# A cross-attention block on one core: the statements of the written-out front, up to the ninth step, in a new order

## The chip, the cores and the metric

The kernel runs on one core of one Trainium2 chip. The metric is the device time of one execution in microseconds (us), and lower is better. A core has a matrix engine (PE in the profile; its weight loads are PEld), three engines for elementwise work (DVE, the vector engine; ACT, the scalar engine; POOL, the general one) and a queue (SP) that here only issues DMA transfers. Each engine works off its own list of instructions in the order of the program and waits on semaphores for the others.

## The reference

One transformer block, for 128 sequences of 128 tokens of width 256, in fp32. Queries come from `x`, keys and values from `ctx`; 16 heads of width 16, a strictly causal mask, a softmax, an output projection, a residual and a layer norm, then a two-layer network of width 1024 with its residual and layer norm.

```python
q = (query @ Wq + bq)    # 16 heads of 16
k = (key @ Wk + bk)
v = (values @ Wv + bv)
scores = einsum('bhqd,bhkd->bhqk', q, k) / sqrt(16)
scores = where(j < i, scores, -1e30)
attn = softmax(scores); attn[:, :, 0, :] = 0
ctx = einsum('bhqk,bhkd->bhqd', attn, v)
x1 = layer_norm(query + ctx @ Wo + bo, ln1_g, ln1_b)
out = layer_norm(x1 + relu(x1 @ W1 + b1) @ W2 + b2, ln2_g, ln2_b)
```

## The kernel before

**Pairs and stages.** The 128 sequences are worked in 64 pairs, numbered from 0. A number such as the 3 in `sums(3, 0, ALL)` is the pair. The second argument of the softmax functions is `hi`: 1 for the later half of the queries, which sees up to 128 keys, 0 for the earlier half, which sees 64. A pair goes through these stages:

- `tokens(p, "x" or "c")` turns a loaded block so that features stand on the partitions (DVE, L289); `project_queries`, `project_keys` (PE, L300) and `values` (PE, L356) are the projections, and `copy_queries`, `copy_keys`, `spread_values`, `stack_values` (ACT, L326, L345, L370, L379) bring them out of the PSUM banks.
- `scores` (PE, L411) or, from pair 4 on, `scores_both` (PE, L440) fill the eight banks of PSUM with scores. `mask` (DVE, L456 or L464) takes them out of the banks and adds the mask; a bank is free for PE's next use only then.
- `maximum` is a maximum on DVE (L475) and a subtraction on POOL (L476); `exponential` is ACT (L483); `sums` is a sum and a reciprocal on DVE (L498, L499) and a multiplication on POOL (L500). From pair 5 on there is another softmax: `exponential_by_head` on ACT (L937) does the subtraction and the sum with the exponential, head by head, and POOL is not needed.
- `turn(p, hi, t)` transposes a third of the weights in 32x32 blocks on DVE (L533) into the tile `turned`. `bring(p, queue, which)` and `bring_all` then move the blocks with 16 DMAs (L552), mostly issued by SP, from `turned` to `brought`. A turn of the next pair may overwrite `turned` only after these transfers have landed. `turn_on_pe` (PE, L569, and ACT, L571) does the same for pairs 0 and 1 without DMAs.
- `weigh` (PE, L586, L596) multiplies `brought` with the values, `context` takes the result out, `attention_out` (PE, L635) is the output projection, `attention_sum` and `stats` (DVE, L683, L650) add the residual and take mean and variance, `deviation` and `shift` (POOL, L657, L732; `scale_and_shift` does both for the second norm) make the scales, `norm1` applies them (ACT, L709).
- `hidden` (PE, L875; ACT, L882) and `second` or `second_half` (PE, L894, L1412) are the two-layer network.

From pair 7 on the products are written with 7 block products in place of 8 (a Strassen-like scheme, PE L1153 and L1364). It needs sums and differences of weight blocks: `combine_weights(w, wc)` makes four 128x128 tiles on POOL, `combine_w1` and `combine_w2` four 128x512 tiles each.

**What sets the order.** The whole body is under `tc.manual_schedule`, so the order of the Python statements is the order on each engine. Statements of pairs 9 to 60 come from one list of keys, `ORDER`, in a loop `step(p)`; a step of that loop works at once on the scores of pair p, the output of pair p-2, and the network of pairs p-3 and p-4. The end of the program is written out. So is its front: some 330 statements, in which the pipeline fills. From `do("weigh", 7)` on (`weigh` of pair 5; `do(key, p)` runs one key of the loop) the front is in the loop's own pieces. `do("weigh", 8)` is `weigh` of pair 6, `do("scores", 8)` are the scores of pair 8, `do("v1", 8)` the first products of its values, `do("eh7", 7)` to `do("el7", 7)` are the exponentials of pair 7 by two heads each. The loop begins with `weigh` of pair 7, at about 185 us.

`empty(n)` puts n no-ops on PE. The list holds 5768 of them before and after the change, and the instructions of each engine are the same set in both.

```python
def sums(p, hi, part):                       # L487
    ...
        nc.vector.tensor_reduce(su, sm[:, part, :], AX.X, ALU.add)      # L498
    nc.vector.reciprocal(rs, su)                                        # L499
    nc.gpsimd.tensor_tensor(sm[:, part, :], sm[:, part, :], ..., ALU.mult)   # L500
...
def bring(p, queue, which, whole=False):     # L544
    for u in which:
        i, j = u // NS, u % NS
        queue.dma_start(brought_all[32 * j : 32 * j + 32, i, at],       # L552
                        turned_all[32 * i : 32 * i + 32, ...])
```

Of the kernel before, what the change touches and what calls it, by code (L numbers as in the profile page):

```python
# [10 lines left out]
ALU = mybir.AluOpType  # L11
# [8 lines left out]
def tile_cross_attention_block(  # L20
# [1842 lines left out]
    tokens(2, "x")  # L1863
    scores(0, 1)
# [15 lines left out]
    project_queries(1)  # L1880
    copy_queries(1)
    values(1)
    mask(0, 0, A)
    ps_bv = fold_values()
    maximum(0, 0, ALL)
    sums(0, 1, ONE)
    exponential(0, 0, ALL)
    spread_values(1)
    tokens(2, "c")
    scores(1, 1)  # L1890
    sums(0, 1, TWO)
    stack_values(1)
    sums(0, 0, ALL)
    add_values(ps_bv)
    turn_on_pe(0, 1, range(0, 1))
    turn_on_pe(0, 1, range(1, 2))
    mask(1, 1, A)
    mask(1, 1, B)
    project_keys(2)
    add_bo(0)  # L1900
# [4 lines left out]
    maximum(1, 1, ONE)  # L1905
    scores(1, 0)
    exponential(1, 1, ONE)
    weigh(0)
    context(0)
    project_queries(2)  # L1910
    maximum(1, 1, TWO)
    mask(1, 0, A)
    mask(1, 0, B)
    maximum(1, 0, ALL)
    attention_out(0)
    copy_keys(2)
    exponential(1, 1, TWO)
    values(2)
    sums(1, 1, ONE)
    tokens(3, "c")  # L1920
    copy_queries(2)
    exponential(1, 0, ALL)
    scores(2, 1)
    attention_sum(0)
    stats(0, states[0]["t1"], 1)
    deviation(0, 1)
    stack_values(2)
    shift(0, 1)
    spread_values(2)
    norm1(0)  # L1930
    sums(1, 1, TWO)
    ps_b1 = fold_norm1()
    turn_on_pe(1, 1, range(0, 1))
    turn_on_pe(1, 1, range(1, 2))
    mask(2, 1, B)
    maximum(2, 1, TWO)
    turn_x1_on_pe(0)
    tokens(4, "x")
    nc.gpsimd.tensor_tensor(be1b_r, be1_r, b2_r, ALU.add)
    sums(1, 0, ALL)  # L1940
    mask(2, 1, A)
    turn_on_pe(1, 1, range(2, 3))
    keep_b1(ps_b1)
    add_b1()
    hidden(0, range(2, 4), None, (2, 3, 4, 0))
    exponential(2, 1, TWO)
    maximum(2, 1, ONE)
    hidden(0, range(0, 2), None, (2, 3, 4, 0))
    scores(2, 0)
    turn_on_pe(1, 1, range(3, 4))  # L1950
    tokens(3, "x")
    mask(2, 0, B)
    turn_on_pe(1, 0, range(0, 1))
    mask(2, 0, A)
    add_bo(1)
    maximum(2, 0, ALL)
    sums(2, 1, TWO)
    exponential(2, 1, ONE)
    turn_on_pe(1, 0, range(1, 2))
    sums(2, 1, ONE)  # L1960
    hidden(0, range(4, 6), None, (2, 3, 4, 0))
    project_queries(3)
    copy_queries(3)
    tokens(4, "c")
    exponential(2, 0, ALL)
    project_keys(3)
    sums(2, 0, ALL)
    turn(2, 1, 0)
    turn(2, 1, 1)
    add_bo(3)  # L1970
    turn(2, 0, 0)
    copy_keys(3)
    hidden(0, range(6, 8), None, (2, 3, 4, 0))
    weigh(1)
    bring(2, nc.sync, EVERY[:8])
    context(1)
    residual1(0)
    scores(3, 1)
    mask(3, 1, B)
# [38 lines left out]
    attention_sum(2)  # L2018
    copy_queries(4)
    load_ahead(2)  # L2020
    load_ahead(4)
    stats(2, states[2]["t1"], 1)
    deviation(2, 1)
    turn(3, 1, 0)
    turn(3, 0, 0)
    turn(3, 1, 1)
    shift(2, 1)
    norm1(2)
    hidden(1, range(4, 6), None, (0, 1, 2, 7))
    hidden(1, range(0, 2), None, (0, 1, 2, 7))  # L2030
    hidden(1, range(2, 4), None, (0, 1, 2, 7))
    bring(3, nc.sync, LATE_FIRST[:3])
    turn_x1(2, between=lambda: bring(3, nc.sync, LATE_FIRST[3:7]))
    hidden(1, range(6, 8), None, (0, 1, 2, 7))
    add_bo(4)
    tokens(6, "x")
    combine_w1()
    tokens(5, "c")
    bring(3, nc.sync, LATE_FIRST[7:])
    scores_both(4)  # L2040
    mask(4, 0, A)
# [12 lines left out]
    exponential(4, 1, TWO)
    sums(4, 0, ALL)
    sums(4, 1, TWO)
    second(1, 1)
    second_sum(1)
    hidden(2, range(2, 4), None, (2, 3, 4, 0))
    residual1(2)  # L2060
    turn(4, 0, 0)
    load_ahead(3)
    copy_keys(5)
    copy_queries(5)
    load_ahead(5)
    turn(4, 1, 0)
    weigh(3)
    hidden(2, range(0, 2), None, (2, 3, 4, 0))
    context(3)
    turn(4, 1, 1)  # L2070
    do("stats2", 7)
    stats(0, states[0]["t2"], 2)
    values(4)
    spread_values(4)
    stack_values(4)
    scores_both(5)
    tokens(6, "c")
# [1025 lines left out]
```

## Time and profile before

| what | value |
|---|---|
| median of 3 runs | 1472.59 us (1471.45 to 1474.57) |
| the profiled execution's own time | 1469.98 us |
| its span, first to last instruction | 1468.2 us |
| busy share of PE, PEld, DVE, ACT, POOL | 99%, 95%, 93%, 89%, 87% |
| mean granted clock of PE | 0.997 |
| front, to the first `weigh` of the loop | 184.8 us |
| one step of the loop on PE | 21.97 us |

The profile is of one execution. Its span leaves out 1.8 us around the program. "Busy" of PE includes time in which a matmul is only on its way through the array, so 99% does not say that nothing could be gained; what PE waits for is told by the waits and the idle times in front of instructions. In the timeline a row begins with the start in us and the duration; in brackets at its end stand the idle time of the engine before it and what ended it. SPq is the issue of a DMA on SP's queue, which is over long before the data has landed.

### The profile page before, as it was taken

The page shows a single profiled execution, that of the slowest core. Times are in us where ns is not written, and L with a number is a line of the kernel's source. Part 1 is how long each engine was busy: PE and PEld are TensorE (multiplying, and loading weights), DVE is VectorE, ACT ScalarE, POOL GpSimd, SP SyncE. Part 2 cuts the span into 40 slices and gives each one's busy share as a digit, 9 for nine tenths or more (in the row PEclk, how much of TensorE's full clock was granted, in tenths as well). Part 3 has the DMA queues.
Part 4 walks back from the last instruction along what each step waited for, and adds up shares of the span by engine and source line. Part 5 has one row for each costly group of instructions (what it writes and reads, how often), then busy time and mean ns, then how long its engine had stood idle before and what let it go on. Part 6 is the DMA issues. An engine that isn't in the chain of part 4 may idle for free.

```text
span 1468.2 us, 62017 instructions
## 1 busy us (share of the span) xinstructions
PE 1447.0 (99%) x20713; PEld 1391.6 (95%) x20713; DVE 1371.9 (93%) x3175; ACT 1303.4 (89%) x5559; POOL 1271.2 (87%) x1872
## 2 busy tenths in 40 slices
PE   8999899999999999999999999999999999999998
PEld 7778799999999999999999999999999999999988
DVE  6987999999999999999999999999999999999767
ACT  5659899999999999999999999999999999999743
POOL 5986898988988988988988998998998998998966
PEclk9999999999999999999999999999999999999999
DMA  8274766766766766766766766766766776774541
GB/s 208 63 143 102 179 154 156 162 157 156 161 160 153 162 158 153 163 160 153 160 158 157 159 158 158 160 158 156 163 157 153 163 161 149 164 158 116 140 103 51
DMA packets 367881, 220.34 MB, mean 150 GB/s; under 512 B 280032, under 2 KB 335584, under 8 KB 367584
## 3 DMA queue, kind: packets, MB, share of 16 engines
q1 hardware_dynamic: 365296, 214.27, 63.8%
q8 instruction: 187, 3.06, 1.0%
q10 hardware_dynamic: 2288, 2.11, 0.7%
q14 instruction: 110, 0.90, 0.2%
HBM read 55.06 MB, written 18.09 MB: 50 GB/s over the span
## 4 chain that ended last, share of the span: by engine, by line
PE 92%; DVE 4%; POOL 1%; DMA 1%; ACT 1%; issue 1%; SPq 0%; DVEq 0%; ACTq 0%; POOLq 0%
PE banks L1153 48%; PE banks L1364 24%; PE banks L440 6%; PE banks L596 4%; PE banks L586 2%; PE banks L300 2%; PE banks L875 2%; PE banks L977 1%; PE banks L635 1%; PE banks L356 1%; DVE sm L464 1%; ACT sm L937 1%; DVE turned L533 1%; PE banks L1050 0%; PE banks L1412 0%
## 5 line engine op out<-in xcount | busy, mean ns | idle before, releaser
L937 ACT ACTIVATE sm<-banks,nmx 128x128 f32<-128x128 f32 x944 | 340.8, 396 | 17.9 <-DVE nmx L1568 14.7
L937 ACT ACTIVATE sm<-sm,nmx 128x64 f32<-128x64 f32 x944 | 325.2, 384 | 1.5 <-DVE nmx L926 1.5
L937 ACT ACTIVATION_READ_ACCUMULATOR sm<-banks,nmx 128x1 f32 x944 | 222.8, 236 | 0.0
L937 ACT ACTIVATION_READ_ACCUMULATOR sm<-sm,nmx 128x1 f32 x944 | 221.8, 235 | 0.0
L533 DVE STREAM_TRANSPOSE turned<-sm 128x1024 f32<-128x1024 f32 x186 | 217.0, 1214 | 3.3 <-DMA brought<-turned 1.8
L1153 PE MATMUL banks<-wt,hS 128*128 128x128 f32 x1344 | 177.7, 275 | 0.0
L1364 PE MATMUL banks<-xS,w1t 128*128 128x128 f32 x1344 | 177.2, 275 | 0.0
L1153 PEld LDWEIGHTS banks<-wt,hS 128*128 128x128 f32 x1344 | 163.6, 192 | 0.1
L1364 PEld LDWEIGHTS banks<-xS,w1t 128*128 128x128 f32 x1344 | 163.4, 192 | 0.0
L1568 DVE TENSOR_REDUCE nmx<-banks 128x4 f32<-128x512 f32 x224 | 152.3, 680 | 1.9
L1557 POOL TENSOR_TENSOR hS<-hT 128x512 f32<-128x512 f32 x116 | 148.2, 1279 | 3.7 <-ACT hT L882 2.4
L1364 PE MATMUL banks<-brought,w 128*128 128x128 f32 x896 | 118.2, 275 | 0.0
L1153 PE MATMUL banks<-w,hT 128*128 128x128 f32 x896 | 109.8, 275 | 0.0
L1364 PEld LDWEIGHTS banks<-brought,w 128*128 128x128 f32 x896 | 109.0, 192 | 0.0
L1618 POOL TENSOR_TENSOR x1b<-x,g_r 128x512 f32<-128x512 f32 x56 | 72.4, 1293 | 39.4 <-ACT x L709 39.4
L1153 PEld LDWEIGHTS banks<-w,hT 128*128 128x128 f32 x896 | 104.8, 192 | 0.1
L440 PE MATMUL banks<-kT,qT 32*64 32x128 f32 (+1 forms) x3840 | 98.3, 331 | 1.8 <-ACT vz L1278 1.5
L1393 ACT ACTIVATE hT<-hT,b1e_c 128x256 f32<-128x256 f32 x224 | 95.7, 510 | 1.2 <-DVE hT L1389 1.1
L1562 DVE TENSOR_TENSOR banks<-banks,neg 128x256 f32<-128x256 f32 x224 | 93.3, 417 | 0.0
L440 PEld LDWEIGHTS banks<-kT,qT 32*64 32x64 f32 x3840 | 79.4, 131 | 12.6 <-ACT vz L1278 1.9
L709 ACT ACTIVATE x<-t,nb,sd 128x256 f32<-128x256 f32 x126 | 68.4, 593 | 19.7 <-POOL nb L732 12.9
L1219 ACT ACTIVATE kr<-banks,b_c 128x128 f32<-128x128 f32 x224 | 83.7, 411 | 1.7 <-PE banks L1153 1.7
(324 smaller groups left out, 4821.5 us busy)
## 6 DMA issues: line engine op xcount, KB each, us to landing
brought<-turned SPq DMA_DIRECT2D x936, 128.0 KB, 2.4
out_dram<-t SPq DMA_DIRECT2D x63, 256.0 KB, 4.0
xb<-in_x_dram SPq DMA_DIRECT2D x124, 128.0 KB, 3.2
cb<-in_ctx_dram SPq DMA_DIRECT2D x124, 128.0 KB, 3.2
x<-in_x_dram SPq DMA_DIRECT2D x56, 256.0 KB, 2.8
kT<-kr SPq DMA_DIRECT2D x112, 128.0 KB, 2.2
brought<-turned SPq DMA_DIRECT2D x40, 96.0 KB, 2.4
w<-in_L_xattn_W_dram SPq DMA_DIRECT2D x2, 1024.0 KB, 7.4
```

What stands on the lines that cost most here:

```text
L440: nc.tensor.matmul(st["sps", hi][r][s * HP : (s + 1) * HP, m * 2 * n : (m + 1) * 2 * n].rearrange("p (e j) -> p e j", e=2), st["qT"][strip ...
L533: nc.vector.transpose(turned[:, :, at : at + 256].rearrange("p j (n a) -> p n j a", a=32), states[p]["sm", hi].rearrange("p h j -> p (h j) ...
L709: nc.scalar.activation(x1[:, s], t1[:, s], AF.Identity, bias=st["nb", 1][:, s], scale=sd[:, s])
L937: nc.scalar.activation(sm[:, h, :], src, AF.Exp, bias=nmx[:, h : h + 1], scale=1.0, **({"accum_out": st["su"][:, at : at + 1]} if summed e ...
L1153: nc.tensor.matmul(out, left(k) if self.depth > 1 else left, right(k) if self.depth > 1 else right, start=(n == 1 and k == 0), stop=(k == ...
L1219: nc.scalar.activation(self.k[:, m, s * P : (s + 1) * P], src, AF.Identity, bias=bk_c[:, m : m + 1], scale=1.0,)
L1364: nc.tensor.matmul(ps[:, i * P : (i + 1) * P].rearrange("p (n a) -> p n a", a=32), left(i), right, start=(n in (1, 2, 5) and i == 0), stop ...
L1393: nc.scalar.activation(self.hT[:, f, at], self.hT[:, f, at] if src is None else src, AF.Relu, bias=b1e_c[:, f : f + 1], scale=1.0,)
L1557: engine.tensor_tensor(c[:, n], left, right, how)
L1562: nc.vector.tensor_tensor(ps[:, :, HP:], ps[:, :, HP:], neg[:, 1, None, :].to_broadcast([P, 4, HP]), ALU.add)
L1568: nc.vector.tensor_reduce(states[p]["nmx", 1][:, 4 * b : 4 * b + 4], banks[:, b].rearrange("p (n j) -> p n j", j=P), AX.X, ALU.max, negate ...
L1618: nc.gpsimd.tensor_tensor(st["x1b"], st["x1b"] if n else st["x1"], (be1b_r if n else g1_r)[:, None, :].to_broadcast([P, 2, D]), ALU.add if ...
```

## The change

The front's statements, from `tokens(2, "x")` up to the loop, stand in a new order. No statement is added or taken away, no size, engine, tile or bank is changed. On SP's queue every DMA stands where it stood; PE, DVE, ACT and POOL have a new order. The loop and the end of the program are the same. The diff has some 330 statements that move; this is its core, with what the prediction speaks of:

```diff
     tokens(2, "x")
+    combine_weights(wv, wvt)
     scores(0, 1)
...
+    combine_weights(wk, wkt)
     values(0)
     stack_values(0)
+    combine_weights(wo, wot)
...
-    tokens(2, "c")
+    tokens(2, "c")
+    tokens(3, "c")
     exponential(0, 0, ALL)
...
     project_keys(2)
-    add_bo(0)
+    copy_keys(2)
     turn_on_pe(0, 1, range(2, 3))
...
-    sums(3, 1, ONE)
-    exponential(3, 0, ALL)
-    attention_out(2)
-    scale_w1()
-    copy_keys(4)
-    sums(3, 1, TWO)
-    sums(3, 0, ALL)
...
+    second_sum(0)
+    exponential(3, 1, ONE)
+    sums(3, 1, ONE)
+    sums(3, 1, TWO)
+    scale_w1()
+    nc.gpsimd.tensor_tensor(b1e_c, b1e_c, b1_c, ALU.add)
+    stats(0, states[0]["t2"], 2)
+    scale_and_shift(0)
+    exponential(3, 0, ALL)
+    sums(3, 0, ALL)
+    context(2)
+    turn(3, 1, 1)
...
-    turn(3, 1, 0)
-    turn(3, 0, 0)
-    turn(3, 1, 1)
-    shift(2, 1)
+    shift(2, 1)
+    turn(3, 0, 0)
+    project_keys(4, 6)
+    copy_keys(4)
+    turn(3, 1, 0)
...
+    hidden(2, range(4, 6), None, (2, 3, 2, 3))
+    hidden(2, range(6, 8), None, (2, 3, 2, 3))
+    weigh(4)
     project_keys(6)
+    copy_keys(6)
+    values(5)
...
-    values(5)
-    copy_queries(6)
-    turn(5, 1, 1)
-    hidden(2, range(6, 8), None, (2, 3, 2, 3))
-    turn(5, 0, 0)
-    combine_weights(wk, wkt)
-    reciprocals(5)
     turn_x1_blocks(3)
-    weigh(4)
...
+    do("kr", 7)
+    do("ks", 7)
+    do("ks2", 7)
+    do("q4", 7)
+    do("qr", 7)
...
+    do("el0", 7)
+    do("vr", 7)
...
+    do("el1", 7)
+    do("el2", 7)
+    do("el6", 7)
+    do("el5", 7)
+    do("xs0", 7)
     do("weigh", 8)
```

On POOL, which is without work from 5 to 20 us, three of the four `combine_weights` now stand ahead of the first softmax; the fourth, `combine_w1` and `combine_w2` move too. On PE the list changes in few places: `weigh` of pair 4 stands ahead of the keys of pair 6 and the values of pair 5, and the hidden layer, the projections and the scores of pairs 2 to 6 change places with one another.

The places of the two pieces that the prediction speaks of, in the order of the engines' lists. A row is a line of the kernel, the operation, the tiles written and read (a number at the end of a name tells tiles of one kind apart), the size and a count.

The first is on POOL, around the last work of the softmax of pair 3 (`sm_3`; `nmx0` and `rs0` are the maxima and reciprocals of the earlier half, `rs1` those of the later one). Before:

```order
L476 TENSOR_TENSOR sm_3_1017<-sm_3_1017,nmx0_3_1110 128x1024
L500 TENSOR_TENSOR sm_3_1017<-sm_3_1017,rs1_3_0_1199 128x1024
L500 TENSOR_TENSOR sm_3_1017<-sm_3_1017,rs1_3_8_1215 128x1024
L500 TENSOR_TENSOR sm_3_1017<-sm_3_1017,rs0_3_0_1220 128x1024
L657 TENSOR_SCALAR ve1_2_1251<-mv1_2_1244 128x2
L658 TENSOR_TENSOR sd1_2_1252<-ve1_2_1251,power_96 128x2
```

The same place on POOL now, where `b1e_c` is a sum of biases and `ve2_0`, `sd2_0`, `nb2_0` are the scales of pair 0's second norm:

```order
L476 TENSOR_TENSOR sm_3_1000<-sm_3_1000,nmx0_3_1087 128x1024
L500 TENSOR_TENSOR sm_3_1000<-sm_3_1000,rs1_3_0_1221 128x1024
L500 TENSOR_TENSOR sm_3_1000<-sm_3_1000,rs1_3_8_1226 128x1024
L2016 TENSOR_TENSOR b1e_c_185<-b1e_c_185,b1_c_116 128x8
L657 TENSOR_SCALAR ve2_0_1241<-mv2_0_1234 128x2
L658 TENSOR_TENSOR sd2_0_1242<-ve2_0_1241,power_96 128x2
L732 TENSOR_SCALAR nb2_0_1245<-mv2_0_1234,sd2_0_1242 128x1 x2
L500 TENSOR_TENSOR sm_3_1000<-sm_3_1000,rs0_3_0_1249 128x1024
L657 TENSOR_SCALAR ve1_2_1273<-mv1_2_1264 128x2
```

Four small operations, among them the scales of pair 0's second norm, have come in ahead of the third multiplication of `sums` of pair 3.

The second is on PE, where the keys of pair 6 (L300) and the values of pair 5 (L356) stood among the matmuls of the hidden layer of pair 2 (L875, with no-ops between them), ahead of `weigh` of pair 4:

```order
 L875 MATMUL banks<-brought,w_132 128x256
 L253 NO_OP x6
-L300 MATMUL banks<-cT_1633,wk 128x256 x4
-L356 MATMUL banks<-wv,cT_1369 128x256 x4
 L875 MATMUL banks<-brought,w_132 128x256
 L253 NO_OP x6
```

And on PE a little further on, at the end of `weigh` of pair 4 (L586, L596) and the second layer of pair 2 (L1412):

```order
 L586 MATMUL banks<-brought,vd_176 32x64 x8
 L596 MATMUL banks<-brought,vz_174 32x64 x16
+L300 MATMUL banks<-cT_1653,wk 128x256 x4
+L356 MATMUL banks<-wv,cT_1346 128x256 x4
 L1412 MATMUL banks<-w_138,hT 128x256 x8
```

The two projections have moved from ahead of `weigh` of pair 4 to behind it.

More of the change, by code (lines that the diff above doesn't have):

```diff
@@ L1909, in tile_cross_attention_block @@
     context(0)
-    project_queries(2)
-    maximum(1, 1, TWO)
-    mask(1, 0, A)
+    exponential(1, 1, TWO)
     mask(1, 0, B)
     maximum(1, 0, ALL)
+    sums(1, 1, ONE)
+    project_queries(2)
+    copy_queries(2)
     attention_out(0)
[L1916 to L1923, printed above, removed]
     attention_sum(0)
     stats(0, states[0]["t1"], 1)
+    scores(2, 1)
     deviation(0, 1)
+    shift(0, 1)
@@ L1927, in tile_cross_attention_block @@
+    sums(1, 1, TWO)
+    exponential(1, 0, ALL)
+    values(2)
     stack_values(2)
-    shift(0, 1)
     spread_values(2)
     norm1(0)
-    sums(1, 1, TWO)
+    add_bo(1)
+    nc.gpsimd.tensor_tensor(be1b_r, be1_r, b2_r, ALU.add)
     ps_b1 = fold_norm1()
+    mask(2, 1, B)
     turn_on_pe(1, 1, range(0, 1))
     turn_on_pe(1, 1, range(1, 2))
-    mask(2, 1, B)
+    turn_x1_on_pe(0)
+    turn_on_pe(1, 1, range(2, 3))
+    mask(2, 1, A)
+    scores(2, 0)
+    hidden(0, range(2, 4), None, (2, 3, 4, 0))
@@ L1936, in tile_cross_attention_block @@
     maximum(2, 1, TWO)
-    turn_x1_on_pe(0)
+    exponential(2, 1, TWO)
     tokens(4, "x")
-    nc.gpsimd.tensor_tensor(be1b_r, be1_r, b2_r, ALU.add)
-    sums(1, 0, ALL)
-    mask(2, 1, A)
-    turn_on_pe(1, 1, range(2, 3))
-    keep_b1(ps_b1)
-    add_b1()
[L1945 to L1952, printed above, removed]
@@ L1953, in tile_cross_attention_block @@
-    turn_on_pe(1, 0, range(0, 1))
[L1954 to L1958, printed above, removed]
+    tokens(3, "x")
+    keep_b1(ps_b1)
+    hidden(0, range(0, 2), None, (2, 3, 4, 0))
+    hidden(0, range(4, 6), None, (2, 3, 4, 0))
+    maximum(2, 1, ONE)
+    exponential(2, 1, ONE)
+    sums(1, 0, ALL)
+    mask(2, 0, A)
+    turn_on_pe(1, 1, range(3, 4))
+    mask(2, 0, B)
+    maximum(2, 0, ALL)
+    exponential(2, 0, ALL)
+    add_b1()
+    sums(2, 1, TWO)
@@ L1959, in tile_cross_attention_block @@
+    turn_on_pe(1, 0, range(0, 1))
     turn_on_pe(1, 0, range(1, 2))
+    project_keys(3)
+    copy_keys(3)
+    project_queries(3)
     sums(2, 1, ONE)
-    hidden(0, range(4, 6), None, (2, 3, 4, 0))
-    project_queries(3)
+    sums(2, 0, ALL)
+    combine_weights(wq, wqt)
+    turn(2, 1, 1)
     copy_queries(3)
[L1964 to L1967, printed above, removed]
+    weigh(1)
     turn(2, 1, 0)
-    turn(2, 1, 1)
-    add_bo(3)
+    scores(3, 1)
+    context(1)
@@ L2060, in tile_cross_attention_block @@
[L2060 to L2065, printed above, removed]
+    scores_both(4)
+    finish_scale(0)
+    mask(4, 0, A)
+    project_queries(5)
+    copy_queries(5)
+    mask(4, 1, A)
+    maximum(4, 1, ONE)
+    exponential(4, 1, ONE)
+    mask(4, 0, B)
+    maximum(4, 0, ALL)
+    mask(4, 1, B)
+    maximum(4, 1, TWO)
+    project_keys(5)
+    second(1, 0, pad=3)
+    sums(4, 1, ONE)
+    copy_keys(5)
+    exponential(4, 0, ALL)
+    sums(4, 0, ALL)
```

574 lines of the change are left out of this document (272 added, 302 removed).

## Prediction

> **What bounds the kernel now.** I read the page first: the shares of the engines and the chain of work that ended last.
>
> ```profile
> span 1468.2 us, 62017 instructions
> PE 1447.0 (99%) x20713; PEld 1391.6 (95%) x20713; DVE 1371.9 (93%) x3175; ACT 1303.4 (89%) x5559; POOL 1271.2 (87%) x1872
> PE 92%; DVE 4%; POOL 1%; DMA 1%; ACT 1%; issue 1%; SPq 0%; DVEq 0%; ACTq 0%; POOLq 0%
> ```
>
> PE carries 92% of the chain, so a new order can pay only where PE waits. Next the chain in order of time, to see where the front ends and what a step of the loop takes.
>
> ```profile
> 185.21 0.45 PE banks L596 x32
> ```
>
> This is a `weigh` of the loop's first step. Everything behind it is the same list in both kernels, so what counts is how late PE, SP, DVE and ACT arrive there. The busy time of PE in three parts of the front says how much there is to win at most (columns: the stretch, its length, busy time and instructions, granted clock, DMA share):
>
> ```profile
> 0.00:35.00 35.00, 31.13 (x295) 0.95 0.88 212
> 35.00:100.00 65.00, 64.09 (x725) 1.00 0.43 96
> 100.00:184.85 84.85, 78.05 (x1033) 1.00 0.64 142
> ```
>
> PE is not busy for 3.87, 0.91 and 6.80 us, 11.6 in all, and some of the first part is the start itself. The waits of the last part by what ended them (total, times, longest):
>
> ```profile
> PE banks L586 <- ACT qT L1181: 1.4, 1, 1.4
> PE banks L440 <- ACT vz L1278: 1.1, 1, 1.1
> PE banks L300 <- DVE sm L464: 1.1, 1, 1.1
> ...
> PE banks L1153 <- ACT kr L1219: 0.8, 1, 0.8
> ...
> PE banks L1153 <- DVE sm L456: 0.5, 1, 0.5
> ```
>
> They are short and come from several engines; no one wait is worth more than 1.4 us (0.1%). The front can move the time by a few us either way, about the 0.2% (2.9 us) that a measurement of this kernel can tell from no change.
>
> **The change part by part.** No instruction comes or goes; each part is a place in a list.
>
> *To 20 us.* POOL has nothing to do ahead of its first subtraction:
>
> ```profile
> 19.99 3.75 POOL L476 TENSOR_TENSOR sm<-sm,nmx 128x1024 f32<-128x1024 f32 x2 [14.86 <-DVE nmx L475]
> ...
> 119.01 0.46 POOL L1105 TENSOR_TENSOR wkt<-wk 128x128 f32<-128x128 f32 x1
> ```
>
> Three `combine_weights` fit into the 14.86 us of idle time, at 4 tiles of 0.46 us each, 5.5 us in all. What hides them is that idle time; without it they would stand ahead of the first softmax with 5.5 us. I cost them at nothing, and nothing is gained at once either, since the places they left on POOL were not waited for.
>
> *28 to 100 us.* The tokens of pairs 2 and 3 go ahead of `sums(0, 0)`, and `copy_keys(2)` ahead of the copies that `turn_on_pe` needs. I walked the lists with the old durations: PE is 1 to 2 us later from 35 us on, and is back to about 0.4 us by the scores of pair 3. PE's idle time there is only 0.91 us, so it can't gain more than that; the bounds are -0.9 and +2, and I take 0, since behind 60 us other engines set the pace.
>
> *POOL and SP at 76 to 118 us.* This is the first term of the sum. The last work of pair 3's softmax on POOL and what follows it:
>
> ```profile
> 76.11 5.62 POOL L500 TENSOR_TENSOR sm<-sm,rs 128x1024 f32<-128x1024 f32 x3
> 81.69 0.23 POOL L657 TENSOR_SCALAR ve<-mv 128x2 f32<-128x2 f32 x1
> ...
> 82.83 0.50 POOL L732 TENSOR_SCALAR nb<-mv,sd 128x1 f32<-128x1 f32 x2
> ...
> 80.64 3.50 DVE L533 STREAM_TRANSPOSE turned<-sm 128x1024 f32<-128x1024 f32 x3 [0.22 <-issue]
> ```
>
> Three multiplications end at 81.69, and the third of the three turns can end at 84.14. In the new order the same three small forms (81.69 to 83.28, 1.6 us, here those of pair 0) and the sum of biases (0.3 with its gap) stand ahead of the third multiplication, and its group starts about 0.4 later: it ends at 81.69 + 1.6 + 0.3 + 0.4 = 84.0. Behind it, DVE's list now has two turns, that of the earlier half, which reads this product, and `turn(3, 1, 0)`; before, one of the three could already be done by then. At 3.50 / 3 = 1.17 each the last ends at 86.4, so 2.25 us later. Now SP:
>
> ```profile
> 84.20 1.83 SPq L552 DMA_DIRECT2D brought<-turned  x3
> ...
> 105.55 10.60 SPq L552 DMA_DIRECT2D brought<-turned  x16
> ...
> 117.99 2.37 DVE L533 STREAM_TRANSPOSE turned<-sm 128x1024 f32<-128x1024 f32 x2 [1.77 <-DMA brought<-turned]
> ```
>
> SP's list does not change, begins with the transfers of the last turn, and issues from 84.20 to 116.15 with no gap (the groups left out lie end to end: the rest of pair 3's sixteen, blocks of x1 and the context of a later pair). So the whole list shifts by 2.25, and the sixteen blocks of pair 4, which have landed shortly ahead of 117.99 (about 117.7), land at about 119.95.
>
> *PE at 113 to 147 us.* PE meets them with `weigh(4)`:
>
> ```profile
> 114.96 1.99 PE L300 MATMUL banks<-cT,wk 128*128 128x256 f32 x8
> 116.79 1.89 PE L356 MATMUL banks<-wv,cT 128*128 128x256 f32 x8
> 118.52 1.89 PE L875 MATMUL banks<-brought,w 128*128 128x256 f32 x8
> 120.34 0.43 PE L586 MATMUL banks<-brought,vd 128*32 128x64 f32 x16
> ...
> 125.47 2.23 PE L440 MATMUL banks<-kT,qT 32*64 32x128 f32 x64
> ...
> 139.66 7.17 PE L875 MATMUL banks<-brought,w 128*128 128x256 f32 x32
> 146.77 1.71 PE L440 MATMUL banks<-kT,qT 32*64 32x128 f32 x64
> ```
>
> Before, the keys of pair 6 and the values of pair 5 (114.96 to 118.52, 3.56 us) covered the wait. Now they stand behind `weigh(4)`: PE is there at about 120.34 - 3.56 + 0.3 = 117.1, waits 2.8 us for the blocks until 119.95, and then still owes 3.56. Against before it is 0.39 us early at `weigh(4)` and 3.17 late behind the two projections. The scores of pair 6 are stretched by mask and values (2.23 us, against 1.71 for the same 64 matmuls of pair 7), and that 0.52 goes, since the later PE finds its banks free. Sum: 3.56 - 0.39 - 0.52 = +2.65 at the hidden layer of pair 3 (142.3 in place of 139.66) and at the scores of pair 7. The bounds are 0, if the shift on POOL and SP does not come, and 3.6.
>
> *147 to 185 us.* Here ACT is the bound (busy time of PE, PEld, DVE, ACT, POOL):
>
> ```profile
> 149.30 0.37 ACT L937 ACTIVATE sm<-banks,nmx 128x128 f32<-128x128 f32 x1 [1.53 <-DVE nmx L1568]
> ...
> 149.30:162.80 13.50, 8.92 (x147) 7.61 (x146) 11.94 (x31) 13.50 (x77) 9.11 (x16) 1.00 0.62 149
> 163.00:185.00 22.00, 21.39 (x248) 20.75 (x252) 21.50 (x50) 19.72 (x88) 19.98 (x32) 1.00 0.81 195
> ```
>
> From the maximum of pair 7 ACT works 13.50 of 13.50 us. It keeps its 77 instructions in another order, so it ends 2.65 later: the copies `kr`, `qr`, `vr`, now ahead of the last exponentials, only change who waits. Behind it, the wait of 0.5 for `sm` L456 goes, as the first layer's products stand ahead of it: 2.65 - 0.5 = 2.15. PE has 0.6 us of idle time in the last stretch, half of which a late PE does not need: about +1.8 at the loop's first step. DVE, busy 21.50 of 22, and SP give nothing back. In the loop PE is the chain, and a late start stays late.
>
> Sum: +1.8 us. Against the profiled execution (1469.98 us, span 1468.2) that is 1471.8; the median of the three runs is 2.6 above that execution, so 1472.59 + 1.8 = 1474.4. By the 0.2% that is no change.
>
> **The rivals.** *Slower, +4 (1476.6).* The mechanism is the same shift of SP's list, reaching one transfer further. In the last step of the front, SP has again no room:
>
> ```profile
> 166.10 11.19 SPq L552 DMA_DIRECT2D brought<-turned  x16
> 177.34 4.12 SPq L92 DMA_DIRECT2D cb<-in_ctx_dram  x4
> ```
>
> If the last turn of pair 7 is 4 us late, so are these, the keys' transfers behind them and the scores of pair 9, and nothing pays it back. That happens from 87.5 us for the last turn of pair 3 on (PE waits 3.9 in place of 2.8 at `weigh(4)`: 3.6 in the sum, with no 0.5 won). For it: every term of the walk up to 100 us was a delay. Against: PE's list gives 0.5 back at two places.
>
> *Faster, -3.3 (1469.3).* If the shift at 84 does not reach `weigh(4)`, the new order of step 7 works from the old time. Then `kr`, `qr` and `vr` ahead of the last exponentials take away the waits of 1.4, 1.1 and 0.8 us, 3.3 in all. Against: ACT has no idle time there, and the third turn waits for the last exponential.
>
> *All absorbed, -0.7 (1471.9).* POOL takes pair 0's scales in a gap, the last turn ends by 84.2, and PE wins only two waits of some 0.4 us.
>
> *The clock, +3.2 (1475.8).* The trace shows one dip of the granted clock, behind PE's waits at the start (1.38 and three of 0.17 us, with two matmuls between each two, from 15.66 to 18.84):
>
> ```profile
> 17.04 0.43 PE L411 MATMUL banks<-kT,qT 32*64 32x128 f32 x2 [1.38 <-DVE sm L464]
> 18.84 0.68 PE L411 MATMUL banks<-kT,qT 32*64 32x128 f32 x26 [0.17 <-DVE sm L464]
> ...
> 20.00:21.00 1.00, 1.00 (x4) 0.82 (x3) 1.00 (x3) 0.00 (x0) 1.00 (x1) 0.50 1.02 418
> ...
> 19.45 3.68 PE L300 MATMUL banks<-cT,wk 128*128 128x256 f32 x8
> 22.93 1.92 PE L300 MATMUL banks<-xT,wq 128*128 128x256 f32 x8
> ```
>
> The clock is 0.50 and eight projections take 3.68 us in place of 1.92, a price of 1.76. If the new wait of 2.8 us at 117 brings such a dip, the sum is 1.8 + 1.4, as part of it falls on `weigh` itself, which is short of work. Against: the waits of 1.4 and 1.1 at 158 to 163 leave the clock at 1.00 in the row of that stretch.
>
> The Trainium skill has a rule for this on the page "TensorE: Matmul & The Clock Gate", section "Part 1: The HAM clock gate (the "warmup" mystery)": an idle window of some 3.4 us halves the clock of the matrix engine, until it was busy for as long. By it a single wait of 2.8 us would not do it, one of 3.9 as in the slower rival could. The trace's dip at 20 us agrees in size (0.50), and no run here shows a wait of 2.8.
>
> **How the numbers follow.** My walk adds some dozen durations by hand, and each crossing of two engines can be off by half a us. Chances: the forecast's case (+0.2 to +2.9) 0.35, all absorbed 0.15, faster 0.20, slower 0.23, the clock 0.07. Faster by more than 2.9 us is 0.20; within 0.2% is 0.35 + 0.15 = 0.50; slower 0.23 + 0.07 = 0.30. The range leaves out the outer halves of the two outer cases: from 1469.0, just under the faster rival's time, to 1478.0, the slower rival's with the clock's price of 1.4. The likeliest case alone goes from 1472.8 to 1475.5.
>
> **What would show it.** In the profile after: the last turn of pair 3 on DVE ends at about 86.4 in place of 84.1, and SP's transfers begin there; `weigh(4)` on PE has a wait of 2 to 3 us, ended by a DMA, at about 119.95; the hidden layer of pair 3 begins near 142.3 with the two projections behind `weigh(4)`; ACT is again without idle time through pair 7's exponentials; the first `weigh` of the loop is 1 to 3 us later than 185; the steps behind it keep their length. I am wrong if the last turn of pair 3 ends by 84.2 or the wait at `weigh(4)` stays under 1 us (then the time falls), if a wait of over 1 us that is not in the list above stands between 147 and 185, or if the loop's steps themselves change.

## The result and the profile after

The changed kernel takes 1479.41 us in the median of 6 runs (1475.67 to 1481.74), against 1471.63 for the kernel before: a ratio of 1.0055 (95% interval 1.0043 to 1.0067), so 6.3 to 9.9 us slower. Timed again later with 5 more runs it was 1476.75, a ratio of 1.0044 (1.0031 to 1.0056). Both together say some 7 us, 0.5%. Two runs of one kernel further down, `after_mid_fixed`, were slow (1830.81 and 2094.01 us), and its ratio is without them. The forecast was 1474.4, with a range that ends at 1478.0.

The head of the page:

```profile
span 1473.9 us, 62017 instructions
PE 1446.5 (98%) x20713; PEld 1388.8 (94%) x20713; DVE 1373.8 (93%) x3175; ACT 1301.8 (88%) x5559; POOL 1269.9 (86%) x1872
PE 89%; SPq 3%; DVE 3%; DMA 2%; POOL 2%; ACT 1%; issue 1%; ACTq 0%; DVEq 0%; POOLq 0%
```

The two later parts of the front (stretch, length, busy time of PE, PEld, DVE, ACT and POOL, granted clock, DMA share, GB/s):

```profile
35.00:100.00 65.00, 63.04 (x651) 50.49 (x650) 59.45 (x92) 40.16 (x78) 55.60 (x49) 1.00 0.41 92
100.00:184.85 84.85, 75.64 (x1007) 65.65 (x1006) 69.22 (x140) 69.42 (x326) 56.65 (x79) 1.00 0.62 138
```

The work is the same; SPq, which had 0% of the chain, now has 3%, and PE idles 1.05 and 2.4 us more in these parts. Of the 5.7 us that this execution's span is longer, 5.53 are lost when the loop's first `weigh` starts (190.31 against 184.78), and from the next one on it stays 5.75. The end of the front in the chain of work that ended last:

```profile
187.18 1.20 DVE turned L533
188.38 0.24 DVE rs L511
188.62 0.56 DVE hT L1383
...
190.38 0.36 PE banks L586 x16
```

From 166 us on PE alone was the chain before; now PE waits for DVE there. The rows that answer to the prediction's, from the timeline of the changed kernel:

```profile
84.53 2.37 DVE L533 STREAM_TRANSPOSE turned<-sm 128x1024 f32<-128x1024 f32 x2 [0.59 <-POOL sm L500]
86.97 1.84 SPq L552 DMA_DIRECT2D brought<-turned  x3
121.10 0.43 PE L586 MATMUL banks<-brought,vd 128*32 128x64 f32 x16 [2.20 <-DMA brought<-turned]
150.49 0.92 PE L440 MATMUL banks<-kT,qT 32*64 32x128 f32 x28
153.02 0.37 ACT L937 ACTIVATE sm<-banks,nmx 128x128 f32<-128x128 f32 x1 [1.52 <-DVE nmx L1568]
166.88 1.25 DVE L533 STREAM_TRANSPOSE turned<-sm 128x1024 f32<-128x1024 f32 x1
170.73 11.91 SPq L552 DMA_DIRECT2D brought<-turned  x16
186.01 2.37 DVE L533 STREAM_TRANSPOSE turned<-sm 128x1024 f32<-128x1024 f32 x2 [2.72 <-DMA brought<-turned]
189.22 1.16 PE L1364 MATMUL banks<-brought,w1t 128*128 128x128 f32 x8 [1.84 <-DVE hT L1383]
```

Pair 3's last turn ends at 86.90, SP begins at 86.97, and `weigh(4)` waits 2.20 us for a DMA: these rows are about where the prediction put them (86.4, 86.4, 2.8). The scores of pair 7 are 3.72 us late, those of pair 8 2.5 (165.48 against 163.00), the first `weigh` of the loop 5.53: step 7 (from the scores of pair 7 to those of pair 8) gives 1.2 back, step 8 (from there to the loop) loses 3.0.

### The profile page after: what moved, and what is told of

Read it like the earlier page. It is cut to its first block, busy times and chain, and to the rows that moved or that the text cites. A ratio compares the mean times of both kernels' runs of the same rounds, so it can differ in the third digit from the quotient of the medians.

```text
span 1473.9 us, 62017 instructions
## 1 busy us (share of the span) xinstructions
PE 1446.5 (98%) x20713; PEld 1388.8 (94%) x20713; DVE 1373.8 (93%) x3175; ACT 1301.8 (88%) x5559; POOL 1269.9 (86%) x1872
## 3 DMA queue, kind: packets, MB, share of 16 engines
q8 instruction: 187, 3.06, 0.9%
## 4 chain that ended last, share of the span: by engine, by line
PE 89%; SPq 3%; DVE 3%; DMA 2%; POOL 2%; ACT 1%; issue 1%; ACTq 0%; DVEq 0%; POOLq 0%
PE banks L1153 48%; PE banks L1364 24%; PE banks L440 6%; PE banks L596 4%; PE banks L586 2%; SPq L552 1%; PE banks L875 1%; SPq L92 1%; PE banks L977 1%; DMA brought<-turned 1%; DMA xb<-in_x_dram 1%; PE banks L356 1%; PE banks L300 1%; PE banks L1412 0%; POOL sm L500 0%
## 5 line engine op out<-in xcount | busy, mean ns | idle before, releaser
L937 ACT ACTIVATION_READ_ACCUMULATOR sm<-banks,nmx 128x1 f32 x944 | 217.3, 230 | 0.0
L937 ACT ACTIVATION_READ_ACCUMULATOR sm<-sm,nmx 128x1 f32 x944 | 214.4, 227 | 0.0
L1589 DVE BATCH_NORM_STATS2 bsa<-t 128x6 f32<-128x256 f32 x224 | 83.1, 413 | 0.1
```

Source lines behind the costliest of these rows:

```text
L937: nc.scalar.activation(sm[:, h, :], src, AF.Exp, bias=nmx[:, h : h + 1], scale=1.0, **({"accum_out": st["su"][:, at : at + 1]} if summed e ...
L1589: nc.vector.bn_stats(states[p]["bs", p][:, at + s], states[q][t][:, s])
```

## The experiments

All are orders of the same statements; "+" is against the kernel before, by the ratio.

**Which part of the front.** Two mixtures with their border behind the scores of pair 7. Against before:

```diff
     do("scores", 7)
+    combine_w2()
+    combine_c(7)
     turn(6, 1, 0)
+    do("oc2", 7)
...
```

> The old order up to the scores of pair 7, the new one from there to the loop. Theory A (the loss comes from POOL and SP at 76 to 118 us and reaches the loop through SP's list): the scores of pair 7 start at about 147 again, and the new order of steps 7 and 8 costs only its own terms, 0.3 us on ACT and 0.6 on DVE ahead of the transfers of pair 7: about +1 us against before. Theory B (the order of steps 7 and 8 itself costs the time, and an early delay would be paid back there): +3 us or more, first weigh of the loop at 188 or later. Theory C (the new order has its loss in the first 60 us or in the clock there): no change, within 1 us.

Measured 1470.42 us, a ratio of 1.000 (0.9989 to 1.0010). The other way round, against the changed kernel:

```diff
     do("scores", 7)
+    residual1(3)
+    finish_shift(0)
     turn_x1_blocks(4)
...
```

> The new order up to the scores of pair 7, the old one from there to the loop. Theory A: the scores of pair 7 start at 150.5 as in the changed kernel (3.7 us late), and the old order of steps 7 and 8 has no more than 1 us to give back: +3 to +5 us against before. Theory B: at most +2 us, since the old order of steps 7 and 8 has its gaps for a late start. Theory C: as the changed kernel, +5 to +8.

Measured 1476.77 us, 1.0039 (1.0024 to 1.0054): +5.7. Theory B falls: nearly all of the loss is made ahead of 147 us. The two numbers fit theory C, which has the loss in the first 60 us; the second is also only just above theory A's +3 to +5. In the trace of the first mixture step 7 gives 1.2 us back and step 8 loses 2.6, as in the changed kernel; its times do not resolve the 1.4 that would be left.

**Ahead of pair 2's weigh, or behind** (some 73 us). Against before:

```diff
     tokens(2, "x")
+    combine_weights(wv, wvt)
     scores(0, 1)
...
```

> The new order up to the weigh of pair 2 (about 73 us), the old one from there on. Theory D (PE itself loses 3 to 4 us between 28 and 60 us, where turn_on_pe of pairs 0 and 1 and the projections behind it wait for ACT and POOL, and the old order later has no gap to pay it back): +3 to +4 us against before. Theory A (the loss comes from POOL and SP at 76 to 118 us): at most +1.

Measured 1474.48 us, 1.0026 (1.0014 to 1.0038): +3.9. About half of the loss lies where the prediction had put 0, and in this trace, which has the clock dip of the kernel before at the same place, every mark from 89 us to the loop is 2.1 to 2.2 us late: nothing gives it back.

```diff
     weigh(2)
+    combine_weights(wv, wvt)
+    combine_weights(wk, wkt)
+    combine_weights(wo, wot)
+    combine_weights(wq, wqt)
     spread_values(3)
-    context(2)
+    project_queries(4)
...
```

> The old order up to the weigh of pair 2, the new one from there on. Theory D: what is left of the loss when the first 73 us are as before, the uncovered wait at weigh(4) and the order on POOL ahead of it: +2.5 to +4.5 us. Theory A: +5 to +8, as the changed kernel.

Measured 1480.30 us, 1.0071 (1.0055 to 1.0087): +10, beyond either theory, and a fault of the mixture: the four `combine_weights` came in ahead of pair 3's sums on POOL (the first and the last of 16 tiles, and the turn that waits for the sums):

```profile
73.85 0.46 POOL L1105 TENSOR_TENSOR wvt<-wv 128x128 f32<-128x128 f32 x1
80.53 0.45 POOL L1108 TENSOR_TENSOR wqt<-wq,wqt 128x128 f32<-128x128 f32 x1
84.73 1.25 DVE L533 STREAM_TRANSPOSE turned<-sm 128x1024 f32<-128x1024 f32 x1 [7.11 <-POOL sm L500]
```

DVE's turn waits 7.1 us for POOL, and SP's transfers of pair 3 left at 90.62, against 84.20 before. This trace has no clock dip in the start and reaches `weigh(2)` 2.1 us earlier than the kernel before; counted from there SP is 8.5 us late and the loop 9.7, near the +10. PE also waits twice for ACT ahead of the scores of pair 4 (2.01 and 1.92 us), and the clock is low from 89 to 96 us, so POOL need not carry all of it. The middle was run again with these sums where the old order has them:

```diff
     weigh(2)
     spread_values(3)
-    context(2)
+    project_queries(4)
...
```

> The new order only from the weigh of pair 2 to the scores of pair 7 (73 to 147 us), the old one ahead and behind, with the sums of weight blocks on POOL where the old order has them. If the prediction's two terms (POOL's order ahead of the last turn of pair 3, and the uncovered wait at weigh(4)) are right in size: +1.5 to +3 us against before, with the last turn of pair 3 ending 2 us later against the weigh of pair 2 and a wait of 2 us at weigh(4). If the +10 of the earlier run with the old start is the middle's own: +8 or more; if it came from the sums of weight blocks alone, which stood there ahead of pair 3's sums, less than +4.

Measured 1473.56 us, 1.0019 (1.0009 to 1.0030): +2.8, as the prediction's two terms have it. Pair 3's last turn is 1.6 us later against `weigh(2)`, and `weigh(4)` waits 2.34. (A wait of 1.41 us for ACT at 75.84, which only the two mixtures with this seam have, is taken up there: `weigh(4)` starts 47.58 us behind `weigh(2)`, 47.34 in the changed kernel.) The new start's 3.9, the middle's 2.8 and 0 for steps 7 and 8 make 6.7, against some 7.

**The start, split at the weigh of pair 0** (about 35 us): first the new order up to there, then the new order from there to `weigh(2)`. Against before:

```diff
     tokens_turned("x")
+    combine_weights(wk, wkt)
     values(0)
     stack_values(0)
-    maximum(0, 1, ONE)
...
```

> The new order up to the weigh of pair 0 (about 35 us), the old one behind it. The wait of 1.25 us at turn_on_pe of pair 0 (ACT copies pair 2's keys first) and that of 0.5 for POOL are in it. If they are passed on: +1.2 to +1.8 us against before. If the old order of 36 to 73 us has a slack for them, as the new order had (where putting the two things back gave 0.1 us at the weigh of pair 2): within 0.5 us of before.

Measured 1471.89 us, 1.0015 (1.0007 to 1.0024): +2.2, passed on. In its own trace, which has no clock dip in the start, PE waits 0.52 us for POOL and 0.51 for ACT at `turn_on_pe`; none of the six traces with the old order there has a wait at that place. In the seven traces of the new order with the dip ahead of this place it is one wait of 1.25 us for ACT, as in `new_to_weigh2`, PE and then ACT:

```profile
33.60 0.66 PE L569 MATMUL banks<-ident,sm 128*128 128x128 f32 x4 [1.25 <-ACT brought L571]
...
31.13 1.93 ACT L345 ACTIVATE kT<-banks,bkh,half 128x256 f32<-128x256 f32 x4 [0.88 <-PE banks L300]
32.95 2.06 ACT L571 COPY brought<-banks 128x512 f32<-128x512 f32 x4
```

The copies of pair 2's keys (L345) hold ACT for 1.93 us ahead of the copies that free `turn_on_pe`'s banks; before, ACT was idle there for 1.53 us, copied at once, and PE had no wait.

```diff
     weigh(0)
-    context(0)
-    project_queries(2)
+    tokens(3, "c")
+    add_bo(3)
+    copy_keys(2)
...
```

> The old order up to the weigh of pair 0, the new one from there to the weigh of pair 2 (without the sums of weight blocks on POOL, which stay where the old order has them), the old one behind. If the loss of the new start lies between 36 and 73 us, where PE waits at turn_on_pe of pair 1 and the queries of pair 3 for ACT (0.2, 0.5, 0.3 and 0.7 us) with less work ahead: +2.5 to +4 us against before, as with the whole new start (+4.0). If it lies ahead of 36 us: at most +1.

Measured 1475.52 us, 1.0033 (1.0022 to 1.0043): +4.9. So the second half of the start loses time by itself. PE in the same timeline of the new start:

```profile
46.83 0.63 PE L569 MATMUL banks<-ident,turned 128*128 128x128 f32 x4 [0.51 <-ACT brought L571]
54.23 1.07 PE L569 MATMUL banks<-ident,turned 128*128 128x128 f32 x8 [0.30 <-ACT hT L882]
57.73 1.99 PE L300 MATMUL banks<-xT,wq 128*128 128x256 f32 x8 [0.70 <-ACT brought L571]
...
61.13 1.12 PE L411 MATMUL banks<-kT,qT 32*64 32x256 f32 x32
62.18 1.99 PE L875 MATMUL banks<-x1T,w 128*128 128x256 f32 x8
```

And the kernel before at the same place:

```profile
57.00 1.89 PE L875 MATMUL banks<-x1T,w 128*128 128x256 f32 x8
...
60.29 1.12 PE L411 MATMUL banks<-kT,qT 32*64 32x256 f32 x32
```

Before, the last part of pair 0's hidden layer (L875) stood ahead of the scores of pair 3 (L411); now it stands behind them. The scores start only 0.84 us later, but PE owes 1.8 us of work that it had done by then. The waits account for the lateness: with the 1.25 us above and one of 0.16, PE waits 2.92 us in this trace from 28 to 73 us, against 0.44 before, and `weigh(2)` starts 2.56 us later (75.28 against 72.72). The two halves of the start, each run alone, make 7.1 us, and the whole start 3.9, so the size of each half is not settled.

**The waits of 28 to 36 us undone**, in the changed kernel:

```diff
-    tokens(2, "c")
-    tokens(3, "c")
     exponential(0, 0, ALL)
...
     sums(0, 0, ALL)
+    tokens(2, "c")
+    tokens(3, "c")
...
-    copy_keys(2)
...
     turn_on_pe(0, 0, range(1, 2))
+    copy_keys(2)
```

> The changed kernel with two things of 28 to 36 us back as they were: the tokens of pairs 2 and 3 behind the sums of pair 0, and the copies of pair 2's keys behind the copies of turn_on_pe of pair 0. Theory D: the two waits of 0.5 us (0.5 and 1.2 where the clock had dipped before) at turn_on_pe go, weigh(0) is 1 us earlier against the first scores of pair 1, and the time 0.5 to 1.2 us shorter than the changed kernel's. If something behind it (turn_on_pe of pair 1) sets the pace anyway: no change against the changed kernel, within 0.3.

Measured 1477.23 us, 1.0047 (1.0032 to 1.0063): not told apart from the changed kernel. Its timeline says where the gain went:

```profile
40.21 1.12 PE L411 MATMUL banks<-kT,qT 32*64 32x256 f32 x32 [0.77 <-ACT qT L326]
...
38.74 1.06 ACT L483 ACTIVATE turned<-turned 128x1024 f32<-128x1024 f32 x1 [1.37 <-POOL turned L476]
```

PE, earlier by then, waits for queries whose copy stands on ACT behind an exponential that waits 1.37 us for POOL. `weigh(2)` starts at 75.31, against 75.43 and 75.28 in two traces of the new start with the same clock dip.

**The cover of weigh(4).**

```diff
+    project_keys(6)
+    copy_keys(6)
+    values(5)
     weigh(4)
-    project_keys(6)
-    copy_keys(6)
-    values(5)
```

> The changed kernel with the keys of pair 6 and the values of pair 5 ahead of weigh(4) again. If the uncovered wait is a term of its own (the prediction's step on PE): the wait of 2.2 us at weigh(4) is filled, the scores of pair 7 start near 148.5 in place of 150.5, and the time is about 2 us shorter than the changed kernel's. If SP's list alone sets the pace from there on: PE is earlier at 143 us, but the transfers of pairs 5 to 7 land as before and less than 0.5 us is left of it at the loop.

Measured 1476.63 us, 1.0031 (1.0020 to 1.0043): 3.5 us below the first measurement of the changed kernel, 1.9 below the second, whose interval it overlaps. The wait is gone from its trace, but a dip of the clock at 112 to 117 us, worth 1.7, stands there: from `weigh(3)` to the scores of pair 7 it takes 47.34 us, against 47.52.

**POOL's order ahead of pair 3's last turn.**

```diff
-    nc.gpsimd.tensor_tensor(b1e_c, b1e_c, b1_c, ALU.add)
-    stats(0, states[0]["t2"], 2)
-    scale_and_shift(0)
     exponential(3, 0, ALL)
     sums(3, 0, ALL)
+    nc.gpsimd.tensor_tensor(b1e_c, b1e_c, b1_c, ALU.add)
+    stats(0, states[0]["t2"], 2)
+    scale_and_shift(0)
```

> The changed kernel with the small work of pair 0 (sum of biases, statistics and scales of its second norm) behind the sums of the earlier half of pair 3 in place of ahead of them. Theory A: the third multiplication on POOL ends near 82.7 in place of 84.5, the last turn of pair 3 near 85 in place of 86.9, SP's list, the wait of PE at weigh(4) and all behind it come 1.9 us earlier: 1.5 to 2 us faster than the changed kernel, the first weigh of the loop at about 188.5. Theories B and C: no more than 0.5 us.

Measured 1478.74 us, 1.0046 (1.0032 to 1.0061): no gain that can be told. The last turn came 0.7 us earlier than in `newfront_old78`, which has the same start (87.87 against 88.57), but the small work now stood ahead of pair 2's first norm, whose blocks SP carries between pair 3's:

```profile
87.93 1.84 SPq L552 DMA_DIRECT2D brought<-turned  x3
94.26 2.86 SPq L552 DMA_DIRECT2D brought<-turned  x4
```

The second group leaves at 94.26; in `newfront_old78` it left at 92.86. Both places together:

```diff
     sums(3, 0, ALL)
     nc.gpsimd.tensor_tensor(b1e_c, b1e_c, b1_c, ALU.add)
     stats(0, states[0]["t2"], 2)
     scale_and_shift(0)
...
+    project_keys(6)
+    copy_keys(6)
+    values(5)
     weigh(4)
```

> The changed kernel with both of the prediction's places back: the small work of pair 0 behind the sums of pair 3, and the keys of pair 6 and the values of pair 5 ahead of weigh(4). If these two carry the middle's part and the rest is the early loss and steps 7 and 8: 2.5 to 4 us faster than the changed kernel, +4 to +5.5 against before. If they are one and the same wait: no faster than with the second alone (1476.6 against 1471.5, +5.2).

Measured 1.0059 (1.0045 to 1.0074): no gain, and no trace of it that could say why. Then pair 0's second norm was put behind pair 2's first, alone and with the cover of `weigh(4)`:

```diff
+    nc.gpsimd.tensor_tensor(b1e_c, b1e_c, b1_c, ALU.add)
     second_sum(0)
...
     norm1(2)
+    stats(0, states[0]["t2"], 2)
+    scale_and_shift(0)
+    norm2(0)
```

> The changed kernel with POOL's order at 76 to 85 us fully as before: the sum of biases ahead of pair 3's sums, statistics, scales and second norm of pair 0 behind the first norm of pair 2. If POOL's order is a term of its own: pair 3's last turn ends 1.9 us earlier against the weigh of pair 2, SP's transfers of pair 3 and 4 as well, the wait at weigh(4) shrinks from 2.2 to under 0.5 us, and the time is 1.5 to 2 us below the changed kernel. If PE's lateness of 2.7 us at the weigh of pair 2 sets when pair 3's turns can end: under 0.7 us.

> The same, with the keys of pair 6 and the values of pair 5 ahead of weigh(4) again. If the two are separate terms: 2.8 + 1.5 = 4 us or more below the changed kernel. If both only answer for the one wait at weigh(4): 2 to 3 us below it, as with the second alone.

Measured 1.0063 (1.0049 to 1.0077) and 1.0073 (1.0056 to 1.0089): slower, if anything, than the changed kernel. My place for the norm was at fault: this was not the old order, as the expectation had it. ACT and PE in the first of the two:

```profile
91.94 1.09 ACT L746 ACTIVATE t<-t,nb,sd 128x256 f32<-128x256 f32 x2 [3.06 <-POOL nb L732]
92.94 1.54 ACT L882 ACTIVATE hT<-banks,b1e_c 128x256 f32<-128x256 f32 x4
...
93.81 1.85 PE L440 MATMUL banks<-kT,qT 32*64 32x256 f32 x30 [2.27 <-ACT hT L882]
```

ACT waits 3.06 us for the norm's scales on POOL, and behind it stands the copy of the hidden layer (L882) that frees the banks for the scores of pair 4. With the whole norm behind pair 3's first norm, near where the old order has its scales on POOL:

```diff
     norm1(3)
+    stats(0, states[0]["t2"], 2)
+    scale_and_shift(0)
+    norm2(0)
+    finish_scale(0)
```

> The changed kernel with pair 0's whole second norm behind the first norm of pair 3 and the sum of biases ahead of pair 3's sums. If POOL's order is a term of its own, as the prediction had it: pair 3's last turn ends 11.5 us behind the start of pair 2's weigh in place of 13.1, no wait of PE in the scores of pair 4, the wait at weigh(4) under 1 us, and the time 1 to 2 us below the changed kernel (1.003 to 1.004 of before). If other things than POOL are due at the same time: not told apart from it (1.0044 to 1.0055).

> The same with the keys of pair 6 and the values of pair 5 ahead of weigh(4). If the middle of the front loses by these two places: what is left is the start and steps 7 and 8, 1.002 to 1.003 of before, 3 us or more below the changed kernel. If the middle loses elsewhere: 1.0035 or more.

Measured 1.0039 (1.0026 to 1.0051) and 1.0044 (1.0030 to 1.0058). In the first, the last turn ends 12.43 us behind the start of `weigh(2)` (13.14 in the changed kernel), and `weigh(3)` is as late as `weigh(2)`, 2.34 and 2.33 us; in `newfront_old78` it was 3.62 and 2.71. So POOL's order is worth 0.7 to 0.9 us in the traces up to there, and `weigh(4)` still waits 1.79. Behind `weigh(4)` the gain is lost again, ACT and then PE:

```profile
124.65 1.09 ACT L746 ACTIVATE t<-t,nb,sd 128x256 f32<-128x256 f32 x2 [1.08 <-POOL nb L732]
130.94 1.27 PE L440 MATMUL banks<-kT,qT 32*64 32x256 f32 x30 [0.28 <-ACT vd L379]
```

The old order has only the scales near here; the norm itself (L746) stands behind ACT's copies for pairs 5 and 6 (at 126.88). Here it stands ahead of them, waits 1.08 us for POOL, and the scores of pair 6, held up by the late copies, take 2.7 us in place of 1.7. From `weigh(4)` to `weigh(5)` it takes 20.09 us, against 19.08 in the changed kernel, so this was not the old order either. The cover on top of it won nothing in the times; its trace loses the same 1.0 us there (16.61 against 15.63 in `after_weigh4_late`) and has dips of the clock at 113 to 117 and 164 to 168.

**Step 8.**

```diff
     do("v1", 8)
-    do("maskB", 8)
...
     do("turni", 7)
+    do("maskB", 8)
```

> The changed kernel with the second mask of pair 8 behind the turn of pair 7's reciprocals again. The transfers of pair 7 start 0.6 us earlier against the last turn of pair 7. If that is what step 8 loses: the turn of pair 8 waits 2.1 in place of 2.7 us and the loop starts 0.6 us earlier. If the wait of the turn is set by how long SP's sixteen issues take and land (11.9 us in place of 11.2): less than 0.3 us.

Measured 1477.06 us, 1.0047 (1.0035 to 1.0059). The wait of 2.72 us ahead of pair 8's turn is gone from its trace, but PE waits for the mask instead:

```profile
176.30 1.16 PE L1153 MATMUL banks<-wt,hS 128*128 128x128 f32 x8 [1.44 <-DVE sm L456]
```

From the scores of pair 8 to the loop's first `weigh` it takes 24.76 us, against 24.83. An earlier mixture had the old front, step 7 new and step 8 old; against `oldfront_new78`:

```diff
     do("scores", 8)
...
-    do("maskB", 8)
     do("recip", 7)
...
```

> The old order up to the scores of pair 7, the new one of step 7, the old one again from behind the scores of pair 8. With both step 7 and 8 new, the scores of pair 8 came 1.2 us earlier against those of pair 7 than before, and the first weigh of the loop 2.6 us later against them. If the mask that step 8's new order puts ahead of the reciprocals' turn is what delays the transfers of pair 7 and the turn behind them: the 1.2 us stay, 1470.2 where before has 1471.5. If SP cannot start earlier for another reason: as before, within 0.5 us.

Measured 1472.22 us, 1.0010 (1.0001 to 1.0019) against before. This trace has no clock dip in the start, so all of it is 1.7 us earlier than before; counted from the scores of pair 7, SP started 0.3 us later (19.65 against 19.33), and DVE waited 3.24 us for an addition on POOL that the mixture has late. It does not say what step 8 costs. The first two mixtures say at least where its loss comes from, SP's transfers of pair 7 in `oldfront_new78` and then in `newfront_old78`:

```profile
165.17 11.72 SPq L552 DMA_DIRECT2D brought<-turned  x16
171.09 11.10 SPq L552 DMA_DIRECT2D brought<-turned  x16
```

With the old front and the new step 8 they begin 5.24 us behind the scores of pair 8, as in the changed kernel (5.25); with the new front, 5.0 us late, and the old step 8 they begin 3.11 us behind them, as before (3.10), and step 8 loses nothing (21.81 us against 21.78). So what step 8 loses in the traces comes with its own order and not with the late start; how much of it reaches the time stays open.

**The changed kernel once more.**

> The changed kernel once more. If its first profile is a lucky execution (clock dip at 8 to 12 us, where the scores wait for the masks anyway): a dip at 18 to 23 us or none, the weigh of pair 2 at 75 us and the first weigh of the loop at 190.5 to 192. If the profile is typical: 73.8 and 190.3 again, and the scatter of 6 us lies elsewhere.

`weigh(2)` starts at 75.71 (73.76 in the first trace), the loop at 192.91 (190.31). The granted clock (third column from the right) in the first trace:

```profile
8.00:12.00 4.00, 3.87 (x10) 3.15 (x11) 0.62 (x2) 1.73 (x4) 3.77 (x10) 0.57 0.91 197
18.00:24.00 6.00, 6.00 (x36) 5.07 (x28) 5.46 (x9) 4.50 (x9) 5.45 (x3) 1.00 0.92 259
```

And in the second:

```profile
8.00:12.00 4.00, 3.94 (x27) 3.19 (x32) 1.63 (x7) 2.14 (x5) 3.84 (x10) 1.00 0.98 200
18.00:24.00 6.00, 5.83 (x43) 4.58 (x44) 5.96 (x9) 2.28 (x4) 4.36 (x3) 0.72 0.81 291
114.00:118.00 4.00, 4.00 (x11) 3.25 (x12) 3.00 (x5) 4.00 (x25) 0.00 (x0) 0.57 0.64 154
168.00:172.00 4.00, 3.11 (x66) 2.70 (x67) 2.65 (x5) 3.36 (x11) 3.54 (x7) 0.65 0.84 246
```

In the first the one dip falls at 8 to 12 us, where PE waits for masks soon after and most of it is hidden; in the second it falls at 18 to 24, ahead of work that PE owes, and is passed on. The dip at 114 costs nothing more, as PE would have waited at `weigh(4)` (0.21 us of wait are left there). So the first profile was a lucky execution, and its 5.7 us understate the change.

## Why the prediction was wrong

**To 20 us: right, as far as seen.** POOL's idle time took the early `combine_weights`; the second scores of pair 0 start between 16.2 and 17.4 us in all nineteen traces of either start.

**28 to 100 us: the step that failed.** It said that PE is 1 to 2 us later from 35 us on and "is back to about 0.4 us by the scores of pair 3", and took 0. The new start alone costs 3.9 us (2.1 to 5.6). A lateness of 1 to 2 us behind `turn_on_pe` was foreseen (a wait of 1.25 measured), and the lateness at those scores was 0.84 us. What was wrong is the conclusion: part of the hidden layer, 1.8 us, had moved from ahead of these scores to behind them. A mark that comes on time with less work done is late by that work. With 3.9 in place of 0 the forecast of 1474.4 would have been 1478.3, still counted from the 1472.59 of the first three runs of the kernel before; all six give 1471.63. The size stays rough: with the same clock dip the new start is 2.2 us late in the traces. A dip at 17 to 23 us stands in 8 of the 13 traces with the new order of the first 35 us and in 2 of the 6 with the old one, too few to say whether the order brings it.

**POOL and SP: the row was right, the price less.** The last turn ended 2.76 us later than before where 2.25 was said, but 1.04 of it stood already at `weigh(2)`, and the old order on POOL ahead of the turn (`after_pool_far`) takes 0.7 us from it.

**weigh(4): right.** A wait of 2.8 us was foreseen, 2.20 was seen (2.34 with the old start), and the middle that holds it costs 2.8 alone, against the sum's 2.65; in the first trace of the changed kernel it takes 2.68 us longer than before (76.73 from `weigh(2)` to the scores of pair 7, against 74.05). That covering it again brings these 2 us is seen in the rows; in the times it is likely in one of the four kernels that have the cover, and not seen in the three others.

**147 us to the loop: mis-sized.** The sum had 0.85 us given back, half a us of it by a wait for `sm` L456 that would go; that wait is still there (0.48 at 153.56). Step 7 gave 1.2 back, but step 8 lost 3.0 in the trace: pair 8's turn waits 2.72 us for the transfers of pair 7, which SP began 4.63 us later than before (170.73 against 166.10) and issued in 11.91 in place of 11.19. The rival "slower", which had 0.23, looked at this place, but put it down to a late turn of pair 7; the two mixtures show that it comes with the new order of step 8, late or not. The prediction's own sign of being wrong, waits of PE of over 1 us between 147 and 185 that its list does not have, is there too: 1.01, 1.07 and 1.21 us, at 161 to 169. In the times the two steps together cost 0 with the old front (1.6 us less to 1.5 more).

**The clock: a rival at 0.07 that was real, mostly at another place.** Between 110 and 128 us the granted clock falls to 0.50 in 8 of the 13 traces that have the new order there, and in none of the 6 that have the old one. In six of the eight it falls ahead of `weigh(4)`, in two behind it. Where no wait hides it, the price is some 1.6 us, close to the 1.76 of the start. In the trace of `mid_only` it stands right behind the wait at `weigh(4)`, as the rival had it:

```profile
118.54 0.43 PE L586 MATMUL banks<-brought,vd 128*32 128x64 f32 x16 [2.34 <-DMA brought<-turned]
120.98 2.63 PE L300 MATMUL banks<-cT,wk 128*128 128x256 f32 x8
```

The argument against it, that waits of 1.4 and 1.1 us at 158 to 163 leave the clock at 1.00, came from one execution; in the trace of `new_to_weigh0`, which has the same wait of 1.4 us, the clock fell right behind it, at 160.

## What to carry to other kernels

Compare two orders at a mark only after counting the work that each has done by then; a mark on time with work moved behind it is late. Undoing one suspect of many seldom brings its share: of nine kernels that put one or two places back, none came below 1.003; in most of their traces another wait stood right behind, in some of them one that the undoing itself had made. Where a new order opens short waits on the matrix engine, add the chance of a clock dip to their price, and judge from several executions.

## What the runs showed of the hardware

The clock of PE halves behind much shorter idle times than I had counted on, and not each time. In the second trace of the changed kernel the dip at 114 us stands behind 3.4 us in which PE was busy for 2.05, with waits of 0.80 and 0.62 us:

```profile
110.40:113.80 3.40, 2.05 (x64) 1.14 (x60) 2.99 (x6) 1.90 (x6) 2.23 (x2) 1.00 0.92 188
```

```profile
113.88 3.12 PE L300 MATMUL banks<-xT,wq 128*128 128x256 f32 x8 [0.62 <-DVE sm L464]
```

The first trace has the same two waits, and no dip:

```profile
111.73 1.99 PE L300 MATMUL banks<-xT,wq 128*128 128x256 f32 x8 [0.62 <-DVE sm L464]
```

The Trainium skill, "TensorE: Matmul & The Clock Gate", section "Part 1: The HAM clock gate (the "warmup" mystery)", says that the monitor's window of some 3.4 us runs freely, and that the moment at which the clock rises at the start therefore depends on where in the window the first matmul lands. The two traces would fit the same for a fall in the middle of a kernel, with the same program and waits and one dip; no run here shows the window itself. The page also gives an idle window as the condition of the half clock, and here the measurement differs: PE was busy for 60% of such a stretch.
